# Latent attention: the outputs of two head groups joined, their sums inverted 128 rows wide and spread back by transfers, in place of transposes on VectorE

## The chip, the cores and the metric

The kernel runs on one core of a Trainium2 chip. The metric is the device time of one execution in microseconds (us). The kernel before takes 3241.66 us, the median of three executions (3239.54 to 3242.97). The core has five instruction streams that matter here: TensorE (PE; its weight loads are shown apart as PEld), VectorE (DVE), ScalarE (ACT), GpSimd (POOL) and SyncE (SP), which issues nearly all transfers (SPq in the profile). Each stream runs its instructions in order; semaphores tie them together.

## The reference, cut to what matters

The whole program is `x + attention(layernorm(x))`, followed by a two-layer local-attention block. Only the first part, a multi-head latent attention over 8 batches of 1024 tokens, is touched:

```python
D_MODEL, D_C, D_R, NH = (256, 128, 32, 16); HD = D_MODEL // NH        # HD = 16
x = L0_attn_x                                    # (8, 1024, 256), float32
c_kv = x @ W_kv_down
k_rope = _rotary_apply(c_kv @ W_k_rope, cos, sin)
k = (c_kv @ W_k_up).reshape(Bb, Tt, NH, HD)
v = (c_kv @ W_v_up).reshape(Bb, Tt, NH, HD)
q = (x @ W_q).reshape(Bb, Tt, NH, HD)
q_rope = _rotary_apply(x @ W_q_rope, cos, sin)
scores = jnp.einsum('bqhd,bkhd->bhqk', q, k)
scores = scores + jnp.einsum('bqr,bkr->bqk', q_rope, k_rope)[:, None]
scores = jnp.where(causal[None, None], -jnp.inf, scores / math.sqrt(HD + D_R))
w = jax.nn.softmax(scores, axis=-1)
attn = jnp.einsum('bhqk,bkhd->bqhd', w, v).reshape(Bb, Tt, D_MODEL)
return attn @ W_o
```

What the change touches is the division by the softmax's sum and the way from the weighted values to `attn @ W_o`.

## The kernel before

**Tiling.** The scores are held transposed: keys lie on the 128 partitions, queries along the free axis. The 16 heads form four groups `g` of four; a matmul of the values (L486) puts head `n` of a group on rows 32n to 32n+31 of a PSUM bank of 512 queries. Of these 32 rows the first 16 are the head's values and row 16 is the sum of its weights, since the value tile carries a column of ones after each head (`VW = 17`). The queries come in two halves, `c = 1` (512 to 1023) and `c = 0`.

**Steps.** The work of one batch is a list of 36 units (`units`, L595): first `c = 1`, groups 0 and 1 (units 0 to 12) and groups 2 and 3 (13 to 25), then `c = 0`, groups 0 and 1 (26 to 30) and groups 2 and 3 (31 to 35). A unit is a block of 128 keys, or two short blocks together. In step `s` the program emits, for each engine in this order: the scores of unit `s` (L453, TensorE) and their exponents (L461, ScalarE, two 128x1024 instructions); the product of unit `s-1` with the exponents of the position scores (`turned`, L475, VectorE, two 128x1024 instructions); the matmuls of unit `s-2` with the values (`values`, L486, TensorE). Then come the pieces of other work that the table `beside` (L542) hangs on step `s`: projections of this batch and of the next one, statistics, and the output matmuls `out_add` (L528) with the sum into `x` on VectorE (L532) and its store (L533). The order of PE, DVE, ACT and POOL is the order in which the program emits them (`manual_schedule`); SP's transfers are placed by the framework, and SP takes them one after another. Step 0 of a batch follows step 35 of the one before without a gap, so the last units of a batch are finished in the first steps of the next. After the last batch eleven steps without units follow.

**The end of a group.** When a group's last unit is through `values` (steps 13 and 14 for the first pair of groups, 26 and 27, 31 and 32, and steps 0 and 1 of the next batch), ScalarE copies the bank to `oaT`. One step later `finished` runs on VectorE: a transpose in blocks of 32x32 (L502), which brings queries to the partitions and a head's 17 numbers beside each other; the reciprocal of the 16 sums per row (L504); the product (L508), which writes 16 columns of each head into a tile shared by the even and the odd group. One step later again, for the odd group, `turn_back` transposes the joined tile (L516) to `oT`, whose 128 rows are the channels of eight heads. `out_add` uses `oT` as the stationary operand against `wout`. The output blocks of `c = 1` hang on steps 31, 35 and 0 of the next batch, those of `c = 0` on steps 6 and 10 of the next batch. In the last batch the `c = 1` blocks are held back to the first step after the units.

**Transfers on SP in this stage.** Per batch there are 16 L368 (256 KB each, `q` spread over partitions) and 16 L383 (128 KB each, the same for `k`), four L533 (256 KB stores of `x`) and two L189 (512 KB loads of `x`). `q` and `k` are cast on ScalarE into a high and a low half; the low half comes from a second matmul (`low`, L353).

Of the kernel before, what the change touches and what calls it, by code (L numbers as in the profile page):

```python
# [36 lines left out]
P = 128  # L37
# [11 lines left out]
VW = HD + 1  # L49
# [33 lines left out]
def preln_mla_local_kernel(  # L83
# [72 lines left out]
    def mla(ctx: ExitStack, verdict):  # L156
# [96 lines left out]

        norms = wp.tile([P, B], F32, name="norms")
# [3 lines left out]
        class Batch:  # L258
# [178 lines left out]
            def start(self):  # L437
                b = self.b
                self.rs = small.tile([P, 2, 4, 16], F32, tag="rs", name=f"rs{b}")
                self.acc, self.onat, self.oTs, self.adds = {}, {}, {}, {}  # L440
# [36 lines left out]
            def values(self, parts, pts):  # L477

                lo, ended = 0, []
                for c, g, kb in parts:  # L480
                    q0, w, _ = self.block(c, kb)
                    if kb == 0:
                        self.acc[g] = pacc.tile([P, 512], F32, tag=f"acc{g % 2}", name=f"acc{self.b}_{c}_{g}")
                    for n in range(4):
                        h = 4 * g + n
                        nc.tensor.matmul(  # L486
                            self.acc[g][32 * n : 32 * n + 32, q0 - c * 512 :],
                            self.v[:, kb, h * VW : h * VW + 32], pts[n // 2][:, n % 2, lo : lo + w],
                            start=(kb == 0), stop=(kb == 4 * c + 3),
                        )  # L490
                    lo += w
                    if kb == 4 * c + 3:
                        oT = late.tile([P, 512], F32, tag="oaT", name=f"oaT{self.b}_{c}_{g}", bufs=2)
                        on_a(oT, self.acc.pop(g))
                        ended.append((c, g, oT))
                return ended

            def finished(self, c, g, oT):


                nat = late.tile([P, 16, 32], F32, tag="onat", name=f"onat{self.b}_{c}_{g}", bufs=2)
                nc.vector.transpose(nat.rearrange("p b d -> p (b d)"), oT)  # L502
                r = self.rs[:, c, g]
                nc.vector.reciprocal(r, nat[:, :, HD])  # L504
                e = g % 2
                if e == 0:
                    self.onat[c, g // 2] = nat
                nc.vector.tensor_tensor(  # L508
                    self.onat[c, g // 2][:, :, HD * e : HD * e + HD], nat[:, :, :HD],
                    r.unsqueeze(2).to_broadcast([P, 16, HD]), ALU.mult,  # L510
                )

            def turn_back(self, c, g):
                if g % 2:
                    t = late.tile([P, 512], F32, tag="oT", name=f"oT{self.b}_{c}_{g}", bufs=3)
                    nc.vector.transpose(t, self.onat.pop((c, g // 2)).rearrange("p b d -> p (b d)"))  # L516
                    self.oTs[c, g // 2] = t
                if (c, g) == (0, 3):
                    verdict(self.rs.rearrange("p c g b -> p (c g b)"), f"a{self.b}")
# [22 lines left out]
        for step, who, *what in (  # L542
# [31 lines left out]
            (31, 0, "out_add", 4, 0), (31, 0, "out_add", 4, 1),  # L574
            (32, 1, "rotary", 1, 3),
            (33, 1, "rotary", 1, 2),
# [33 lines left out]
        line, done, turning = [], [], []  # L610
        with tc.manual_schedule(engines={E.PE, E.DVE, E.Activation, E.Pool}):
            for b in range(B + 1):
                for step in range(len(units) if b < B else 11):
# [23 lines left out]
                    if turning:  # L637
                        bt, e = turning.pop(0)
                        bt.turn_back(*e)
                    if done:  # L640
                        bt, e = done.pop(0)
                        bt.finished(*e)
                        turning.append((bt, e[:2]))
                    done += ended
# [1245 lines left out]
```

## Time and profile before

| | |
|---|---|
| time, median of 3 | 3241.66 us (3239.54 to 3242.97) |
| the profiled execution | 3241.02 us |
| its span in the trace | 3239.2 us |
| latent attention | about 0 to 945 us, a batch every 111.4 us |
| local attention and its feed-forward | about 945 to 3239 us |

The profile is of one execution. A busy share counts the time in which an engine had an instruction; TensorE's ends are modelled, so a full TensorE may still have slack. A row of a timeline gives the start, the duration (of neighbouring like instructions together), the engine, the line of the kernel, the operation, the tiles, shapes, the count and, in brackets, how long the engine stood idle before it and what ended that.

The groups of the changed part, over the whole stage on VectorE (line, operation, count, busy time, mean):

| line | what | count | busy us | mean ns |
|---|---|---|---|---|
| L475 | product with the position exponents, 128x1024 | 576 | 672.5 | 1219 |
| L502 | transpose to queries on partitions, 128x512 | 64 | 45.0 | 703 |
| L504 | reciprocal, 128x16 | 64 | 16.2 | 254 |
| L508 | product with the reciprocals, 128x256 | 64 | 27.2 | 425 |
| L516 | transpose back, 128x512 | 32 | 22.5 | 704 |

### The profile page before, as it was taken

Reading aid. Unit: us, or ns where it says so; the run is one execution under the profiler, and the core shown is the slowest. Engines: PE = TensorE matmul, PEld = TensorE weight load, DVE = VectorE, ACT = ScalarE, POOL = GpSimd, SP = SyncE. Lnnn points to the kernel's source line nnn. Section 1 sums busy time; section 2 is a strip of 40 time slices with the busy share of each in tenths; the row PEclk is TensorE's granted clock in tenths of the full one; section 3 lists DMA queues with packets and bytes.
Section 4 is the critical chain, followed back from the end, with each engine's and each line's share of the span. In section 5 each row is a group of like instructions: output and inputs, shape, how many; then the busy total and the mean of one; then the engine's idle time right before and its main releaser. Section 6 shows DMA issues by size and latency. Waiting matters only on the chain.

```text
span 3239.2 us, 112711 instructions
## 1 busy us (share of the span) xinstructions
PE 3159.7 (98%) x50210; PEld 1462.9 (45%) x50210; DVE 2648.5 (82%) x3934; ACT 1734.7 (54%) x2183; POOL 1355.6 (42%) x1065
## 2 busy tenths in 40 slices
PE   7999999999987999999999999999999999999998
PEld 2434444434333454444454444445444444454454
DVE  4999999999988888787888877787877788787773
ACT  6888888888742434444444444443444444444441
POOL 1111010100027655555655654555565555555540
PEclk9999999999998999999999999999999999999999
DMA  4133222422434354544445446455544545454431
GB/s 134 43 93 86 63 73 76 105 51 68 114 95 108 108 132 123 135 112 126 126 118 132 115 130 158 119 136 139 148 123 130 134 122 141 131 147 122 117 107 56
DMA packets 389901, 364.21 MB, mean 112 GB/s; under 512 B 158703, under 2 KB 337310, under 8 KB 389278
## 3 DMA queue, kind: packets, MB, share of 16 engines
q1 hardware_dynamic: 387422, 354.51, 41.3%
q8 instruction: 396, 6.49, 0.8%
q10 hardware_dynamic: 1984, 2.41, 0.2%
q14 instruction: 99, 0.81, 0.1%
HBM read 165.96 MB, written 140.51 MB: 95 GB/s over the span
## 4 chain that ended last, share of the span: by engine, by line
PE 91%; DVE 4%; DMA 2%; ACT 1%; POOL 1%; SPq 1%; issue 1%; DVEq 0%; ACTq 0%
PE ag L668 18%; PE pair L668 13%; PE psy L668 10%; PE acc L486 9%; PE psw L668 7%; PE sc L453 6%; PE pv L668 6%; PE o L1001 6%; PE pair L960 5%; PE psR L201 2%; PE psx L201 2%; PE psq L201 2%; PE s L1009 2%; PE psc L201 1%; PE psrq L201 1%; PE psv L201 1%
## 5 line engine op out<-in xcount | busy, mean ns | idle before, releaser
L475 DVE TENSOR_TENSOR pt<-pt,er 128x1024 f32<-128x1024 f32 x576 | 672.5, 1219 | 13.4 <-ACT pt L461 13.1
L668 PE MATMUL ag<-d,l 128*32 128x512 f32 x5632 | 639.6, 593 | 1.5 <-DVE xs L1041 1.1
L904 POOL TENSOR_TENSOR t<-t,t 128x1024 f32<-128x1024 f32 x128 | 304.2, 2376 | 798.4 <-DVE t L900 798.4
L461 ACT ACTIVATE pt<-sc 128x1024 f32<-128x1024 f32 x576 | 561.8, 1035 | 92.7 <-PE sc L453 83.3
L966 ACT ACTIVATE pt<-pair 128x1024 f32<-128x1024 f32 (+1 forms) x256 | 235.2, 969 | 537.4 <-PE pair L960 480.2
L668 PE MATMUL pair<-l_qkv,xT 128*32 128x512 f32 x4096 | 468.7, 597 | 3.6 <-DMA xT<-zx 2.6
L126 POOL TENSOR_TENSOR rn<-ss,half 128x16 f32<-128x16 f32 x128 | 373.0, 2914 | 13.8
L486 PE MATMUL acc<-pt,v 128*32 128x512 f32 (+3 forms) x3072 | 342.3, 496 | 6.4 <-DVE pt L475 6.3
L668 PEld LDWEIGHTS ag<-d,l 128*32 128x32 f32 x5632 | 177.4, 110 | 373.9 <-issue 354.3
L895 ACT ACTIVATE sq<-pair 128x1024 f32<-128x1024 f32 x128 | 131.3, 1026 | 352.7 <-issue 299.9
L668 PE MATMUL psy<-l,hid 128*32 128x256 f32 x5120 | 282.1, 379 | 0.0
L668 PEld LDWEIGHTS pair<-l_qkv,xT 128*32 128x32 f32 x4096 | 130.9, 111 | 305.9 <-issue 281.4
L453 PE MATMUL sc<-q,k 32*128 32x512 f32 (+3 forms) x3072 | 248.8, 381 | 8.5 <-ACT pt L461 8.3
L897 DVE TENSOR_TENSOR t<-pair,l_cos 128x1024 f32<-128x1024 f32 x128 | 156.0, 1219 | 121.6 <-ACT sq L895 121.3
L418 POOL TENSOR_SCALAR_AFFINE_SELECT er<-er 128x128 f32<-128x128 f32 x64 | 51.1, 802 | 481.1 <-ACT er L416 481.1
L1133 DVE SCALAR_TENSOR_TENSOR hid<-ag,l_b,ge 128x512 f32<-128x512 f32 x160 | 116.8, 730 | 162.6 <-ACT ge L1132 93.4
L910 POOL TENSOR_TENSOR t<-t,rn 128x1024 f32<-128x1024 f32 x128 | 243.5, 1902 | 10.0
L1001 PEld LDWEIGHTS o<-pt,v 128*32 128x32 f32 x7680 | 215.1, 110 | 66.2 <-issue 53.2
L668 PE MATMUL pv<-l_qkv,xT 128*32 128x512 f32 x2048 | 243.8, 592 | 0.0
L668 PE MATMUL psw<-l_o,oT 128*32 128x256 f32 x4096 | 236.5, 382 | 0.7 <-DVE xs L1170 0.7
L1019 DVE RECIPROCAL rs<-s 128x256 f32<-128x256 f32 x128 | 223.2, 1744 | 16.2 <-PE s L1009 16.2
L1001 PE MATMUL o<-pt,v 128*32 128x128 f32 x7680 | 234.5, 273 | 1.7 <-POOL pt L968 1.6
(326 smaller groups left out, 4595.9 us busy)
## 6 DMA issues: line engine op xcount, KB each, us to landing
z<-turned SPq DMA_DIRECT2D x512, 128.0 KB
qkT<-z SPq DMA_DIRECT2D x128, 512.0 KB
y<-xs SPq DMA_DIRECT2D x128, 128.0 KB
h<-y SPq DMA_DIRECT2D x32, 512.0 KB
zx<-turneds SPq DMA_DIRECT2D x120, 128.0 KB
xT<-zx SPq DMA_DIRECT2D x240, 64.0 KB
zh<-turnedh SPq DMA_DIRECT2D x120, 128.0 KB
d<-zh SPq DMA_DIRECT2D x30, 512.0 KB
```

The lines of the kernel that those rows point to most:

```text
L126: nc.gpsimd.tensor_tensor(out_, in_, half[:, :n], ALU.pow)
L201: nc.tensor.matmul(out[four], w[:, four], rhs, start=start, stop=stop)
L453: nc.tensor.matmul(two[n // 2][:, n % 2, lo : lo + w], k[rows], q[rows, h], start=(h == 1), stop=(h == 0),)
L461: nc.scalar.activation(pt, sc, AF.Exp, scale=SCALE)
L475: nc.vector.tensor_tensor(t, t, er.to_broadcast([P, 1024 // w, w]), ALU.mult)
L486: nc.tensor.matmul(self.acc[g][32 * n : 32 * n + 32, q0 - c * 512 :], self.v[:, kb, h * VW : h * VW + 32], pts[n // 2][:, n % 2, lo : lo + w],
L668: nc.tensor.matmul(out[four], w[:, four], rhs, start=start, stop=stop)
L904: nc.gpsimd.tensor_tensor(t1, t1, t2, ALU.add)
L910: nc.gpsimd.tensor_tensor(t1, t1, rn.unsqueeze(3).to_broadcast([P, 2, HEADS, DH]), ALU.mult)
L966: nc.scalar.activation(pt[:, :, : n * P], flat[:, :, : n * P], AF.Exp, scale=-1.0)
L1001: nc.tensor.matmul(o[32 * j : 32 * j + 32, g, a, :], vs[m][:, h * DH + a * 32 : h * DH + a * 32 + 32], pts[m][g][:, place(j), off : off + ...
L1019: nc.vector.reciprocal(rs, s)
```

## The change

The value matmul of an odd group takes its 32 columns of the value tile 16 earlier: its values then fall on rows 16 to 31 of each head's 32 rows and, since the column before a head is a column of ones, the sum falls on row 15. For an even group nothing moves. ScalarE copies an even group's bank straight into `oT` and an odd group's into a tile `odd`. SP then moves, for each group, the four rows of sums (512 numbers each) to 32 rows of 16 in a small tile `rs`; for the odd group it also moves the four blocks of 16 value rows over `oT`'s rows 16 to 31. Two steps after the odd group's end, `inverse` takes the reciprocal of both groups' sums at once on VectorE (128x32), SP stores them to DRAM (`zr`), and eight loads spread each row of 512 over the 16 partitions of its head (`by`). Four steps after the odd group's end, `scaled` multiplies `oT` by `by` on VectorE. In the table of other work the first output block of `c = 1` moves from step 31 to step 33, and a position block (`rotary 1, 2`) from step 33 to step 31.

```diff
+        zrs = [dram.tile([2, 4, 32, 16], F32, tag=f"zr{i}", name=f"zr{i}") for i in range(2)]
...
-                self.rs = small.tile([P, 2, 4, 16], F32, tag="rs", name=f"rs{b}")
-                self.acc, self.onat, self.oTs, self.adds = {}, {}, {}, {}
+                self.rs = small.tile([P, 2, 2, 2, 16], F32, tag="rs", name=f"rs{b}")
+                self.acc, self.by, self.oTs, self.adds = {}, {}, {}, {}
...
+                    at = HD * (g % 2)
...
-                            self.v[:, kb, h * VW : h * VW + 32], pts[n // 2][:, n % 2, lo : lo + w],
+                            self.v[:, kb, h * VW - at : h * VW - at + 32], pts[n // 2][:, n % 2, lo : lo + w],
...
-                        oT = late.tile([P, 512], F32, tag="oaT", name=f"oaT{self.b}_{c}_{g}", bufs=2)
-                        on_a(oT, self.acc.pop(g))
-                        ended.append((c, g, oT))
+                        self.ended(c, g)
+                        ended.append((c, g))
...
-            def finished(self, c, g, oT):
-                nat = late.tile([P, 16, 32], F32, tag="onat", name=f"onat{self.b}_{c}_{g}", bufs=2)
-                nc.vector.transpose(nat.rearrange("p b d -> p (b d)"), oT)
-                r = self.rs[:, c, g]
-                nc.vector.reciprocal(r, nat[:, :, HD])
+            def ended(self, c, g):
                 e = g % 2
-                if e == 0:
-                    self.onat[c, g // 2] = nat
-                nc.vector.tensor_tensor(
-                    self.onat[c, g // 2][:, :, HD * e : HD * e + HD], nat[:, :, :HD],
-                    r.unsqueeze(2).to_broadcast([P, 16, HD]), ALU.mult,
-                )
-
-            def turn_back(self, c, g):
-                if g % 2:
-                    t = late.tile([P, 512], F32, tag="oT", name=f"oT{self.b}_{c}_{g}", bufs=3)
-                    nc.vector.transpose(t, self.onat.pop((c, g // 2)).rearrange("p b d -> p (b d)"))
+                if e:
+                    t = late.tile([P, 512], F32, tag="odd", name=f"odd{self.b}_{c}_{g}")
+                else:
+                    t = late.tile([P, 512], F32, tag="oT", name=f"oT{self.b}_{c}_{g}", bufs=4)
                     self.oTs[c, g // 2] = t
-                if (c, g) == (0, 3):
-                    verdict(self.rs.rearrange("p c g b -> p (c g b)"), f"a{self.b}")
+                on_a(t, self.acc.pop(g))
+                for n in range(4):
+                    row = 32 * n + HD - e
+                    nc.sync.dma_start(
+                        self.rs[32 * n : 32 * n + 32, c, g // 2, e], t[row : row + 1].rearrange("o (p f) -> o p f", f=16)
+                    )
+                if e:
+                    for n in range(4):
+                        rows = slice(32 * n + HD, 32 * n + 32)
+                        nc.sync.dma_start(self.oTs[c, g // 2][rows], t[rows])
+
+            def inverse(self, c, m):
+                r = self.rs[:, c, m]
+                nc.vector.reciprocal(r, r)
+                z = zrs[m]
+                nc.sync.dma_start(z.rearrange("e n p f -> (n p) e f"), r)
+                t = self.by[c, m] = late.tile([P, 512], F32, tag="by", name=f"by{self.b}_{c}_{m}", bufs=2)
+                for n in range(4):
+                    for e in range(2):
+                        lo = 32 * n + HD * e
+                        nc.sync.dma_start(
+                            t[lo : lo + HD], z[e, n].rearrange("p f -> (p f)").partition_broadcast(HD)
+                        )
+                if (c, m) == (0, 1):
+                    verdict(self.rs.rearrange("p c m e f -> p (c m e f)"), f"a{self.b}")
+
+            def scaled(self, c, m):
+                t = self.oTs[c, m]
+                nc.vector.tensor_tensor(t, t, self.by.pop((c, m)), ALU.mult)
...
-            (31, 0, "out_add", 4, 0), (31, 0, "out_add", 4, 1),
+            (31, 1, "rotary", 1, 2),
             (32, 1, "rotary", 1, 3),
-            (33, 1, "rotary", 1, 2),
+            (33, 0, "out_add", 4, 0), (33, 0, "out_add", 4, 1),
...
-                    if turning:
-                        bt, e = turning.pop(0)
-                        bt.turn_back(*e)
-                    if done:
-                        bt, e = done.pop(0)
-                        bt.finished(*e)
-                        turning.append((bt, e[:2]))
-                    done += ended
+                    for what in due:
+                        what[0] -= 1
+                    while due and due[0][0] == 0:
+                        due.pop(0)[1]()
+                    for bt, (c, g) in ended:
+                        if g % 2:
+                            due.append([2, lambda bt=bt, c=c, g=g: bt.inverse(c, g // 2)])
+                            due.append([4, lambda bt=bt, c=c, g=g: bt.scaled(c, g // 2)])
+                            due.sort(key=lambda what: what[0])
```

## The prediction

> **What bounds the kernel now.** I read the page's shares first, then its busy time by stretch, then VectorE's order of time inside the attention stage, last the queue of transfers (SPq).
>
> ```profile
> PE 3159.7 (98%) x50210; PEld 1462.9 (45%) x50210; DVE 2648.5 (82%) x3934; ACT 1734.7 (54%) x2183; POOL 1355.6 (42%) x1065
> ```
>
> TensorE looks full over the whole span, but its ends are modelled. The changed code lies in the first 945 us, so the share there decides. These rows give start:end, length, then busy time of PE, PEld, DVE, ACT, POOL for the last two thirds of one batch:
>
> ```profile
> 426.00:470.00 44.00, 43.39 (x499) 17.26 (x502) 41.45 (x53) 37.99 (x50) 5.60 (x6) 1.00 0.21 49
> 470.00:512.00 42.00, 42.00 (x491) 17.32 (x483) 40.67 (x56) 34.56 (x46) 4.47 (x6) 1.00 0.20 52
> ```
>
> A batch takes 111.4 us (the L533 store of 476.64 returns at 588.02), and VectorE has 105 us in it. From 470 to 512 it is the fuller of the two eltwise engines, at 40.67 of 42. In order of time it runs without a gap:
>
> ```profile
> 494.08 0.70 DVE L502 STREAM_TRANSPOSE onat<-oaT 128x512 f32<-128x512 f32 x1
> 494.82 0.25 DVE L504 RECIPROCAL rs<-onat 128x16 f32<-128x16 f32 x1
> 495.11 0.42 DVE L508 TENSOR_TENSOR onat<-onat,rs 128x256 f32<-128x256 f32 x1
> 495.46 2.35 DVE L475 TENSOR_TENSOR pt<-pt,er 128x1024 f32<-128x1024 f32 x2
> ...
> 501.37 0.71 DVE L516 STREAM_TRANSPOSE oT<-onat 128x512 f32<-128x512 f32 x1
> ...
> 509.22 2.35 DVE L475 TENSOR_TENSOR pt<-pt,er 128x1024 f32<-128x1024 f32 x2
> 511.49 0.68 DVE L532 TENSOR_TENSOR x<-psx,x 128x512 f32<-128x512 f32 x1
> ```
>
> The reader is to see that here the group work that the change removes stands between two L475, and that L475 is what the next `values` matmul (L486) waits for. The exponent of the unit that L475 takes at 509.22 started at 504.55: VectorE is 3.6 us behind. At steps 9 and 18 of a batch (407.5, 434.5) it starts within 0.03 us of the first exponent's end. So TensorE and ScalarE set the pace in most steps (about 3.0 us each), VectorE in the last five steps of a batch and the first seven of the next. TensorE's own work in the stretch from the scores of step 31 (472.16) to those of step 7 of the next batch (511.41) is some 3.2 us less than its 39.25 us: steps 34, 4, 5 and 6 took 4.0, 4.1, 3.2 and 4.4 us, for matmuls of 3.3, 3.1, 2.4 and 3.7.
>
> **What is removed and added on VectorE.** Per batch go eight L502 (0.703), eight L504 (0.254), eight L508 (0.425) and four L516 (0.704): 13.9 us. Four reciprocals of 128x32 come; between 0.254 us for 16 columns and 1.744 us for 256 (L1019) a straight line gives 0.35. Four products of 128x512 come, 0.67 by L1024's row. That is 4.1 us, so 9.8 us of work less. In steps with no VectorE lag this is worth nothing: what hides it is the exponents. In the stretch above it is worth at most the 3.2 us that TensorE could save.
>
> **What is added on SP.** Each pair of groups issues 4+4 sum rows, 4 odd-row moves, 1 store of the inverses and 8 spreading loads: 21 transfers, 84 per batch. Rows for the price of an issue:
>
> ```profile
> 5.54 7.45 SPq L226 DMA_DIRECT2D wout<-in_L_attn_W_o_dram  x8
> ...
> 501.16 5.42 SPq L383 DMA_DIRECT2D k<-alves_place_k(1, 0)_6163  x4
> ```
>
> ```profile
> 963.27 1.77 SPq L931 DMA_DIRECT2D z<-turned  x4
> 967.08 0.34 SPq L935 DMA_DIRECT2D qkT<-z  x1
> ```
>
> L226 has 16 partitions like the spreading loads; its unhindered issues follow each other every 0.47 us (0.42 and a gap), L931's every 0.44. I take 0.47. The ends are 0.28 (the one-row stores of L690: 0.83 for three) and 1.27 (the fourth L368 of a burst). The second fence also prices a store to DRAM and the load that waits for it: the last L931 ends at 965.04 and L935 starts at 967.08, 2.04 later, 2.4 from its start; the same wait was 3.7 us for a 256 KB L533 before L189 (414.13 to 417.79). By the semaphore increments in the trace, an L226 load landed 1.9 us after its start. So I take 2.4 for the store and 1.9 for a last landing, with 3.7 as the upper end of each.
>
> One chain is then: copy; four sums (3 x 0.47 + 1.9 = 3.3); reciprocal 0.35; store 2.4; eight loads (7 x 0.47 + 1.9 = 5.2); product 0.7. That is 12 us, for a slot four steps after the copy. `scaled` stands in VectorE's order ahead of the next L475, so when it waits, L475 and then L486 wait behind it.
>
> [...]
>
> **The four pairs of a batch**, on the clock of the batch above, in the order in which the changed kernel's instructions are built:
> - Keys half 1, groups 0 and 1 (copy at step 14, about 424): loads land at 435.9, VectorE arrives near 434, next L475 at 436.6 instead of 434.5. Its L486 runs at 439.3 anyway. 0 us, at worst 1.
> - Groups 2 and 3 (copy ends 464.0): SP still owes three pieces of `k`, so sums leave 464.4 to 466.3, odd rows to 468.2, and four pieces of the next batch's `k` stand ahead of the store, to 470.5. Store lands 472.9, loads leave 473.0 to 476.8, the last lands 478.2. VectorE has ended unit 30's L475 at 475.25: 3.0 us of waiting, unit 31's L475 at 478.9 instead of 476.53, its first half ready at 480.1. TensorE wants it at 478.3 (the change exchanges 1.7 us of output matmuls in step 31 for 0.86 of position matmuls). About 2 us late; the second output block now follows in step 33.
> - Half 0, groups 0 and 1: copy 478.4, reciprocal at its slot 486.6, landing 494.6, VectorE there at 492.6. It waits 2.0, unit 0's L475 starts 495.3; TensorE wants its first half at about 496.2. Hardly a loss: TensorE stays 2.1 behind.
> - Half 0, groups 2 and 3: store at about 503, but the loads stand behind three pieces of `k` (L383), one of which needs the low halves that ScalarE casts in step 4: 504.4 before, 505.3 now. Loads leave 506.4 to 510.1 and land at 511.6; product till 512.3. Step 6's output matmuls read it at once:
>
> ```profile
> 508.76 2.30 PE L201 MATMUL psx<-wout,oT 128*32 128x256 f32 x30
> ```
>
> They now start at 512.3, last 1.7, and the scores of step 7 begin at 514.4 instead of 511.41. **A transition costs 3.0 us**, the whole saving being eaten by the waits. The `q` and `k` that SP delays are wanted eight or more steps later, and cost nothing.
>
> There are seven transitions: 21 us. The last batch has no next one to hide behind:
>
> ```profile
> 936.36 0.70 DVE L502 STREAM_TRANSPOSE onat<-oaT 128x512 f32<-128x512 f32 x1
> ...
> 939.17 5.16 PE L201 MATMUL psx<-wout,oT 128*32 128x256 f32 x56 [6.08 <-DVE oT L516]
> ```
>
> There VectorE loses 6.8 us of group work after 899, gains 2.0, and waits some 3: the last copy comes at about 931.3 instead of 933.3. From it the bare chain counts, with two loads of the next stage between: sums 935.2, store 937.9, loads out 938.8 to 942.6, landing 944.1, product 944.8. The 5.16 us of matmuls start at 944.8 instead of 939.2, before the next stage's first: 5.7 us.
>
> Sum: 7 x 3.0 + 5.7 = 26.7. The span of 3239.2 becomes 3266; the profiled execution's 3241.02 becomes 3267.7, and as it lies 0.6 below the median of 3241.66, I forecast **3268 us**.
>
> Bounds of a transition: with the last pair alone waiting, the cast of step 4 would fall at 501.8 and step 7 at 510.8, -0.6; with 0.28 an issue -1.9; no wait at all -3.2. With 3.7 for store and landing, upstream 3.1 later and 1.8 more at the end: +6 or so, as part of it meets lag that is already there.
>
> **Rivals.**
> 1. The chain is short enough (faster). Place: `scaled` at steps 31, 0 and 5. Price: 3.2 us a transition, and nothing in the last batch, where 3 us of waits and 2.3 of issues fall from the 5.7: 3241.7 - 22.4 = 3219. It decides where the last load lands before VectorE arrives, so if the chain is 3 us shorter than my 12 (0.28 an issue gives 2.0 of it). For it: VectorE's gapless 470 to 512; an engine that is behind finds its loads landed. Against: step 6's matmuls are gated by `k`'s place in SP's order, whatever VectorE does.
> 2. A wash: only that last gate acts, -0.6 x 7 + 5.7 = +1.5, so 3243. For it: the half-0 pair before it costs me almost nothing already.
> 3. SP becomes the bound. Three pairs fall between 455 and 513: 63 x 0.47 = 30 us beside the 17 us of `q`, `k` and stores, 47 of 58. At 1.27 each it would be 97, about 39 too many, less SP's free stretch after it: some +20 a transition, 3390. Against: 1.27 was seen for 256 KB transfers in a burst, while these move 2 to 32 KB.
>
> **Chances.** Forecast 0.62, rival one 0.20, the wash 0.12, SP as bound 0.06. Beyond 0.2% (6.5 us, about what three runs can tell from no change) that makes faster 0.20, same 0.12, slower 0.68. The forecast's own range is 3248 (where sameness ends) to 3296: +6 a transition, and in the tail 5.7 + 4.9 with 3.7 for its store and its two landings, give 3294. Down to 3222 the wash and the upper half of rival one come in; the rest below, and SP as bound, are what is left out.
>
> **What will show it.** In the page after: VectorE's busy time down by about 78 us with the span up; idle time before the new 128x512 product, released by the loads, near 3.0, 2.0 and 2.4 us at steps 31, 0 and 5; SP issues every 0.47 us; step 7's scores 3 us later in each batch. If instead the product starts without idle time, or the batch is under 111.4 us, the chain's length is what I had wrong; if SP never stands idle from 455 to 513, the third rival is right.

## The result, and the profile after

The changed kernel takes 3363.3 us, the median of five executions (3361.41 to 3367.48), against 3241.66 us for the kernel before in the same session: a ratio of 1.0384, 95% interval [1.0373, 1.0396]. The forecast was 3268 us, with a range of its own of 3248 to 3296 (down to 3222 with the wash and part of the first rival). The direction is right, the size is not: 121.6 us are lost where 26.7 had been worked out.

From the page after, the engines' busy time and the engines' shares of the chain of waits, then these shares from the page before:

```profile
PE 3186.7 (95%) x50210; PEld 1474.7 (44%) x50210; DVE 2582.8 (77%) x3774; ACT 1732.5 (51%) x2183; POOL 1358.6 (40%) x1065
...
PE 76%; DMA 8%; DVE 6%; SPq 5%; ACT 2%; issue 2%; POOL 1%; DVEq 0%; ACTq 0%
```

```profile
PE 91%; DVE 4%; DMA 2%; ACT 1%; POOL 1%; SPq 1%; issue 1%; DVEq 0%; ACTq 0%
```

VectorE is 65.7 us less busy, and the span is 126.5 us longer (3365.7). The chain now passes through transfers (DMA, 8%) and through SP's issuing (SPq, 5%); both were at 2% or less. The groups of instructions say who stood still (busy time, mean ns of one, idle time just before them, and what ended it); the second fence is the values' matmul before:

```profile
L488 PE MATMUL acc<-pt,v 128*32 128x512 f32 (+3 forms) x3072 | 347.6, 512 | 50.9 <-DVE pt L476 49.9
L538 DVE TENSOR_TENSOR oT<-oT,by 128x512 f32<-128x512 f32 x32 | 22.1, 692 | 127.5 <-DMA by<-zr 89.7 <-DMA rs<-oT 37.8
L523 DVE RECIPROCAL rs<-rs 128x32 f32<-128x32 f32 x32 | 11.2, 348 | 35.5 <-DMA rs<-odd 35.5
```

```profile
L486 PE MATMUL acc<-pt,v 128*32 128x512 f32 (+3 forms) x3072 | 342.3, 496 | 6.4 <-DVE pt L475 6.3
```

`scaled` (L538) waits 127.5 us in 32 uses for the spread inverses. The row puts 37.8 of these down to `rs<-oT`, moves that SP issues just behind the loads; in the one at 546.74 below, the last spreading load had landed 0.2 us earlier (at 546.52, by the counts of the semaphore that tells of a landing), so there too the loads are what it waits for. The reciprocal (L523) waits 35.5 us for the sums, and the values' matmuls (L488) have 50.9 us of idle time before them, where they had 6.4.

VectorE's order of time over one transition, the changed instructions alone:

```profile
516.12 0.35 DVE L523 RECIPROCAL rs<-rs 128x32 f32<-128x32 f32 x1 [1.62 <-DMA rs<-odd]
527.78 0.69 DVE L538 TENSOR_TENSOR oT<-oT,by 128x512 f32<-128x512 f32 x1 [6.03 <-DMA by<-zr]
538.62 0.34 DVE L523 RECIPROCAL rs<-rs 128x32 f32<-128x32 f32 x1
546.74 0.69 DVE L538 TENSOR_TENSOR oT<-oT,by 128x512 f32<-128x512 f32 x1 [1.93 <-DMA rs<-oT]
554.16 0.34 DVE L523 RECIPROCAL rs<-rs 128x32 f32<-128x32 f32 x1
567.15 0.69 DVE L538 TENSOR_TENSOR oT<-oT,by 128x512 f32<-128x512 f32 x1 [5.26 <-DMA by<-zr]
```

The waits of `scaled` at steps 31, 0 and 5 are 6.03, 1.93 and 5.26 us; forecast were 3.0, 2.0 and 2.4. Over all seven transitions they are 5.8 to 6.7, 0.9 to 2.6 and 3.8 to 7.2. SP's order over the same stretch:

```profile
510.51 1.82 SPq L384 DMA_DIRECT2D k<-alves_place_k(0, 0)_5763  x3
512.42 2.45 SPq L513 DMA_DIRECT2D rs<-odd  x4
514.92 2.49 SPq L519 DMA_DIRECT2D oT<-odd  x4
517.83 2.83 SPq L384 DMA_DIRECT2D k<-alves_place_k(0, 1)_5864  x4
520.75 0.54 SPq L525 DMA_DIRECT2D zr<-rs  x1
522.68 3.62 SPq L530 DMA_DIRECT2D by<-zr  x8
...
553.27 3.15 SPq L369 DMA_DIRECT2D q<-alves_place_q(1, 1)_6312  x4
556.52 1.11 SPq L525 DMA_DIRECT2D zr<-rs  x1
557.73 3.10 SPq L384 DMA_DIRECT2D k<-alves_place_k(1, 0)_6379  x3
561.72 3.55 SPq L530 DMA_DIRECT2D by<-zr  x8
```

The reader is to see the distance between the reciprocal and its store. The reciprocal of 516.12 is done at 516.47, and the store `zr` leaves at 520.75: 4.3 us, in which SP issues odd rows and four pieces of `k` that came earlier in its order. Four on-chip moves take 2.45 us, a transfer every 0.62.

TensorE's order of time, its two gaps in this transition:

```profile
529.67 2.20 PE L488 MATMUL acc<-pt,v 128*32 128x512 f32 x6 [4.67 <-DVE pt L476]
...
567.89 2.79 PE L201 MATMUL psx<-wout,oT 128*32 128x256 f32 x24 [5.24 <-DVE oT L538]
```

And the windows around the second gap (start:end, length, busy time of PE, PEld, DVE, ACT and POOL, the granted clock, the DMA share, GB/s):

```profile
563.00:567.00 4.00, 0.00 (x0) 0.00 (x0) 0.00 (x0) 2.02 (x3) 0.43 (x3) 0.85 0.38 88
567.00:571.00 4.00, 3.11 (x25) 1.28 (x25) 3.21 (x4) 0.00 (x0) 0.00 (x0) 0.50 0.01 2
571.00:575.00 4.00, 4.00 (x33) 1.43 (x32) 4.00 (x5) 2.99 (x4) 0.00 (x0) 0.79 0.65 165
```

This was in no step of the forecast: after the gap TensorE is granted half its clock (0.50), and it is back at full speed 6.8 us after the clock fell (565.84 to 572.66). In the middle of the stage (up to 870 us) the clock records of the trace add up to 78.5 us at half clock; the kernel before has none there.

Where in a batch the time is lost is told by ScalarE's exponents: the interval from the first exponent of a unit to that of the next, as a mean over the second to the seventh batch, less the same interval of the kernel before. The table sums these over stretches of units, in us per batch, for all kernels that were run (a batch before takes 111.4).

| kernel | units 31-34 | 35-3 | 4-8 | 20 | others | batch |
|---|---|---|---|---|---|---|
| after | +7.18 | +0.82 | +5.49 | +1.36 | +0.04 | +14.89 |
| 1: product by a constant | -0.69 | +1.22 | +2.37 | 0.00 | +0.02 | +2.93 |
| 2: matmuls in the gaps | +6.03 | +1.20 | +2.96 | +1.66 | 0.00 | +11.85 |
| 3: later product | -1.77 | +3.95 | +2.22 | 0.00 | +0.77 | +5.17 |
| 4: one spreading load | +6.28 | -0.07 | +5.17 | +0.78 | +0.12 | +12.29 |
| 5: 10 transfers, not 21 | +1.17 | -0.15 | +2.33 | +0.99 | +0.17 | +4.51 |
| 6: 10 transfers, later | -1.79 | +1.17 | -2.29 | 0.00 | +0.77 | -2.14 |
| 7: as 6, one unit more | -1.86 | +1.17 | -2.01 | 0.00 | +0.79 | -1.90 |
| 8: reciprocal of a constant too | -0.69 | -0.22 | +5.91 | 0.00 | +0.05 | +5.05 |
| 9: as 7, last batch as before | -1.86 | +1.17 | -2.21 | 0.00 | +0.75 | -2.15 |
| 10: as 8 without on-chip moves | -0.69 | -0.42 | -1.95 | 0.00 | +0.01 | -3.05 |

### The profile page after: what moved, and what is told of

It reads as the page before. It is cut to its first block, busy times and chain, and to the rows that moved or that the text cites. A ratio compares the mean times of both kernels' runs of the same rounds, so it can differ in the third digit from the quotient of the medians.

```text
span 3365.7 us, 113703 instructions
## 1 busy us (share of the span) xinstructions
PE 3186.7 (95%) x50210; PEld 1474.7 (44%) x50210; DVE 2582.8 (77%) x3774; ACT 1732.5 (51%) x2183; POOL 1358.6 (40%) x1065
## 4 chain that ended last, share of the span: by engine, by line
PE 76%; DMA 8%; DVE 6%; SPq 5%; ACT 2%; issue 2%; POOL 1%; DVEq 0%; ACTq 0%
PE ag L688 18%; PE pair L688 12%; PE psy L688 9%; PE psw L688 6%; PE pv L688 6%; PE o L1021 6%; PE acc L488 5%; PE pair L980 4%; PE sc L454 3%; DVE pt L476 2%; SPq L530 2%; ACT pt L462 2%; PE psx L201 2%; DMA zr<-rs 2%; PE s L1029 2%
## 5 line engine op out<-in xcount | busy, mean ns | idle before, releaser
L488 PE MATMUL acc<-pt,v 128*32 128x512 f32 (+3 forms) x3072 | 347.6, 512 | 50.9 <-DVE pt L476 49.9
L454 PE MATMUL sc<-q,k 32*128 32x512 f32 (+3 forms) x3072 | 253.7, 387 | 11.4 <-ACT pt L462 11.2
L1039 DVE RECIPROCAL rs<-s 128x256 f32<-128x256 f32 x128 | 223.1, 1743 | 15.7 <-PE s L1029 15.6
```

Source lines behind the costliest of these rows:

```text
L454: nc.tensor.matmul(two[n // 2][:, n % 2, lo : lo + w], k[rows], q[rows, h], start=(h == 1), stop=(h == 0),)
L488: nc.tensor.matmul(self.acc[g][32 * n : 32 * n + 32, q0 - c * 512 :], self.v[:, kb, h * VW - at : h * VW - at + 32], pts[n // 2][:, n % 2, ...
L1039: nc.vector.reciprocal(rs, s)
```

## The experiments

Theory A: the waits of the product for the spread inverses hold TensorE, and the half clock after each gap adds to it. The rivals: SP's queue and the traffic cost by themselves (B); the clock costs nothing (C); the waits only move (D); landing, not issuing, decides (E). Times are medians, ratios are to the kernel before on the same chip.

### 1. The product by a constant

```diff
-                nc.vector.tensor_tensor(t, t, self.by.pop((c, m)), ALU.mult)
+                self.by.pop((c, m))
+                nc.vector.tensor_tensor(t, t, wout.rearrange("p n d -> p (n d)"), ALU.mult)
```

> The product of the joined outputs is taken with a constant of the same size (the output weights) in place of the spread inverses, so the inverse sums are left out of the output; every transfer, the reciprocal and the product stay. What goes is the product's wait for the spreading loads. Theory A (that wait holds TensorE, about 4.7 us twice a batch at steps 31 and 5, and the half clock after each gap takes 3.4 us more, 16 us a batch in all): 3363 - 8 x 16 = 3235, between 3215 and 3260; half-clock time falls from 163 us to 50-60. Rival B (the 21 transfers of a pair load the queue of SP and the memory, so the next batch's loads and bfloat16 weights come late): no less than 3330, since they are all still there.

3275.55 us, 1.0107 [1.0090, 1.0124]. This is above A's 3260 and well below B's 3330. The kernel leaves the inverse sums out of its output. A batch loses 2.93 us instead of 14.89, so the product's wait is 12.0 of the 14.9 us. The half clock up to 870 us falls from 78.5 to 13.7 us (over the whole execution from 163.4 to 80.9, where 50 to 60 were expected). What is left shows in VectorE's waits between 150 and 850 us (total, times, longest):

```profile
DVE rs L523 <- DMA rs<-odd: 52.8, 23, 4.2
```

In the changed kernel this was 19.2 us in 10 times: with the product's wait gone, the reciprocal waits for the sums instead. ScalarE waits too: once in each of these batches its cast of `q(0, 0)` stands for 4.5 to 5.5 us until the pieces of `q(1, 1)` have left; run 8 takes this up.

### 2. Matmuls in the gaps

```diff
...
+                if parts[0] == (0, 2, 0):
+                    warm = bank(f"warm{self.b}")
+                    for _ in range(5):
+                        times(warm, wout[:, 0, :P], wout.rearrange("p n d -> p (n d)"), True, True)
...
+                if t == i == 0:
+                    for _ in range(10):
+                        times(ps[:, 0], wout[:, 0, :P], wout[:, 0, :], True, True)
```

> Matmuls whose results are overwritten are put into TensorE's two gaps: five of 512 columns ahead of the values of unit 31 and ten of 256 columns ahead of the output matmuls of step 7, some 4.3 us each at full clock; waits, transfers and VectorE's work are as in the changed kernel. Theory A (half clock after each gap costs 3.4 us, twice a batch): TensorE has more work and the kernel is faster, 3363 - 8 x 6 = 3315, between 3300 and 3335, with the half-clock time near 60 us. Rival C (only the waits count, the lower clock falls in time that is lost anyway): 3363 or above, up to 3400 where the added matmuls run past the end of the waits.

3344.47 us, 1.0325 [1.0307, 1.0343]: 19 us faster than the changed kernel, with some 9 us more of matmuls in every batch. TensorE's order shows the added work in the place of the gap, and the rest of the wait behind it:

```profile
515.46 4.50 PE L201 MATMUL warm<-wout 128*32 128x512 f32 x40
520.94 1.76 PE L492 MATMUL acc<-pt,v 128*32 128x512 f32 x6 [0.98 <-DVE pt L476]
```

There is no half clock left in the middle of the stage. C falls: the clock does cost. But A's 3300 to 3335 is missed too: the batch gains 14.89 - 11.85 = 3.0 us, half of what A had put down. That VectorE, late by the same wait, would have held TensorE in most of the slow time anyway is a reading that no run shows by itself.

### 3. The later product

```diff
-                            due.append([4, lambda bt=bt, c=c, g=g: bt.scaled(c, g // 2)])
+                            due.append([6, lambda bt=bt, c=c, g=g: bt.scaled(c, g // 2)])
...
-            (6, -1, "out_add", 0, 0), (6, -1, "out_add", 0, 1), (6, 0, "low"), (6, 1, "normalise", 0, 3),
+            (6, 0, "value", 3), (6, 0, "low"), (6, 1, "normalise", 0, 3),
...
-            (9, 0, "value", 3), (9, 0, "low"), (9, 1, "normalise", 1, 2),
+            (9, -1, "out_add", 0, 0), (9, -1, "out_add", 0, 1), (9, 0, "low"), (9, 1, "normalise", 1, 2),
...
+            (35, 0, "out_add", 4, 0), (35, 0, "out_add", 4, 1),
```

> The product is due six units after the pair's end in place of four, and what reads it moves behind: the output groups of the second half batch to steps 35 and 0/1 of the next batch, those of the first to steps 9 and 10, one value step and two rotary blocks change places with them. Transfers and work are the same, each with 6 us more to land. Theory A: both gaps go, 3363 - 128 = 3235 less what the reciprocal and product save VectorE, 3210 to 3250. Rival B (SP's queue and the traffic are the cost): over 3300, since the queue is as full. Rival D (the waits only move: the output groups meet the query and value steps and their bfloat16 copies): 3260 to 3320, with gaps of over 3 us before lines other than the values.

3295.41 us, 1.0169 [1.0152, 1.0186]. A's 3210 to 3250 is missed; the time lies in D's range and just under B's bound. The stretch of units 31 to 34 is mended (+7.18 becomes -1.77) and so is unit 20; units 4 to 8 keep 2.22 of 5.49, and units 35 to 3 lose more than they did (+3.95, of which run 6, with the same table of other work, keeps 1.17). VectorE's waits:

```profile
DVE rs L523 <- DMA rs<-odd: 28.8, 18, 3.0
...
DVE oT L538 <- DMA by<-zr: 11.9, 8, 2.4
DVE rs L523 <- DMA oT<-odd: 11.6, 4, 3.5
...
DVE oT L538 <- DMA rs<-oT: 8.0, 4, 2.5
```

The product's wait has shrunk to 19.9 us (11.9 and 8.0) from 89.5 in the same stretch of the changed kernel; the sums come late, because on SP they stand behind the spreading loads of the pair before. ScalarE's cast of `q(0, 0)` waits here as well, 2.7 to 4.0 us in five of six batches, for pieces of `q(1, 1)`. Two units more do not mend it while SP has 21 transfers for each pair.

### 4. One spreading load

```diff
-                for n in range(4):
-                    for e in range(2):
...
+                nc.sync.dma_start(
+                    t, z.rearrange("n e p f -> (n e) (p f)").unsqueeze(1).to_broadcast([8, HD, 512])
+                )
```

> The eight spreading loads of a pair become one transfer with the same bytes, the store of the inverses two in place of one, so that the last load is issued 7 x 0.46 - 0.5 = 2.7 us earlier. Theory A, with SP's issue time as the price: both waits of the product shrink by 2.7 us, from 6.0 and 5.3 to 3.3 and 2.6; with the gaps at TensorE then near 2 us no half clock follows: 16 - 4 = 12 us a batch less, 3265; if the half clock still follows, 8 x 5.4 = 43 less, 3320. Rival E (the time from issue to landing decides, and one big transfer lands later than eight small ones, or the loads stand behind other traffic): 3350 or above.

3348.80 us, 1.0338 [1.0321, 1.0356], only 14.5 us less than the changed kernel, just short of E's 3350; both of A's figures, 3265 and 3320, are missed, and 68.3 of the 78.5 us at half clock remain. That no half clock follows a gap near 2 us was the author's estimate, and it was not shown. SP's order shows where the rest stays:

```profile
505.51 2.49 SPq L519 DMA_DIRECT2D oT<-odd  x4
508.10 3.60 SPq L384 DMA_DIRECT2D k<-alves_place_k(0, 1)_5786  x4
511.80 1.21 SPq L526 DMA_DIRECT2D zr<-rs  x2
514.45 0.63 SPq L528 DMA_DIRECT2D by<-zr  x1
```

The reciprocal here ran from 506.64 to 506.99, and its store waited until 511.80 for its turn: 4.8 us. A product that waits starts 3.9 us (median) after the one load's issue, and 2.1 us after the last of the eight in the changed kernel. So of the 3.0 us of issuing that are saved (eight loads took 3.6 us, one takes 0.63) the landing gives 1.8 back, and the second store 0.6.

### 5. Ten transfers for a pair in place of 21

Beside the one spreading load, a group's four sums go to DRAM in one transfer and come back 128 rows wide in one.

```diff
-                for n in range(4):
-                    row = 32 * n + HD - e
...
+                nc.sync.dma_start(zss[m][e], t[HD - e : P : 32])
                 if e:
...
+                    nc.sync.dma_start(self.rs[:, c, m], zss[m].rearrange("e n (p f) -> (n p) e f", f=16))
```

> A pair of groups issues 10 transfers in place of 21: each group's four sums go to DRAM in one, come back 128 rows wide in one, the inverses go out in two and are spread in one; the odd rows keep their four. SP's issue time per pair falls from about 12 x 0.63 + 0.5 + 8 x 0.46 = 11.7 us to about 10 x 0.55 = 5.5 us, but the sums now make a round trip through DRAM (some 2 x 1.8 us) in place of one landing. Theory A with SP's issue time as the price: 3348 (one spreading load, measured) less 0 to 3 us a batch, 3322 to 3350. Rival E (each transfer's time from issue to landing decides, and there are now more of them in a row): the reciprocal waits some 2 us longer in every pair, four times a batch of which two or three reach TensorE, 3370 to 3400.

3293.59 us, 1.0159 [1.0141, 1.0177]. This is better than either theory: 55 us less than with one spreading load, for an exchange of eight on-chip moves for three transfers that make a longer way. SP's order:

```profile
599.65 1.23 SPq L385 DMA_DIRECT2D k<-alves_place_k(0, 1)_7142  x2
600.98 1.18 SPq L525 DMA_DIRECT2D zr<-rs  x2
603.59 0.63 SPq L527 DMA_DIRECT2D by<-zr  x1
```

The reciprocal of this pair ran from 599.69 to 600.04 and the store leaves at 600.98: 0.9 us instead of 4.8. For the pairs at this place the first seven batches show 0.8 to 2.0 us here and 3.4 to 5.1 in run 4. E falls: the chain has one landing more and is faster. What fell is the time that its links stand in SP's order; eight on-chip moves held SP for some 5 us, the three transfers in their place hold it for 1.6.

### 6 and 7. Both, and one unit more

Run 6 is run 5 with the places of run 3; run 7 has the reciprocal three units after the pair's end and the product seven.

```diff
-                            due.append([2, lambda bt=bt, c=c, g=g: bt.inverse(c, g // 2)])
-                            due.append([6, lambda bt=bt, c=c, g=g: bt.scaled(c, g // 2)])
+                            due.append([3, lambda bt=bt, c=c, g=g: bt.inverse(c, g // 2)])
+                            due.append([7, lambda bt=bt, c=c, g=g: bt.scaled(c, g // 2)])
```

> The 10 transfers of the run before together with the later product and the later output groups. Theory A: what is left in the run with the later product alone (5.1 us a batch more than before: waits of the reciprocal and of the product for loads that stand behind other transfers on SP) goes in part, 3295 - 8 x 3 = 3270, between 3245 and 3290. Rival E: the reciprocal's longer wait costs what the product's gains, 3290 to 3330.

> The same 10 transfers and places of the output groups, the reciprocal three units after the pair's end in place of two and the product seven in place of six: one more unit (3 us) for the sums to land. Theory A with the reciprocal's wait as the rest: VectorE waits nowhere for a transfer in the middle of the stage, a batch takes 111.4 - 2.7 (the steps 4, 31, 34 and 35 that the changed kernel already does faster) = 108.7 to 111.4, and the time is 3240 less 0 to 19 plus 12 to 18 at the end of the last batch, 3235 to 3260. Rival E: over 3280.

3245.24 us, 1.0017 [1.0007, 1.0026], and 3242.34 us, 1.0009 [1.0000, 1.0019]. A holds in both, run 6 at the lowest end of its 3245 to 3290. The unit more takes the reciprocal's wait between 150 and 850 us from 30.8 us in 18 times to 0.2 in one, yet the batch gets no shorter (-2.14 and -1.90): in run 6 VectorE waited where TensorE did not need it. The windows of one batch, of the changed kernel and then of run 6, in two fences:

```profile
542.60:669.30 126.70, 115.24 (x1288) 47.55 (x1288) 97.03 (x111) 96.44 (x129) 11.69 (x14) 0.95 0.34 81
```

```profile
479.50:589.10 109.60, 108.73 (x1285) 45.24 (x1288) 96.36 (x112) 96.56 (x128) 14.37 (x14) 1.00 0.38 94
```

The same matmuls; 11.5 us without them and a clock of 0.95 in the first, 0.9 us without them and a full clock in the second. A batch is now 2 us shorter than the kernel before has it. Nothing of that reaches the whole: the end of the stage, where no next batch hides the chain, takes it back. From the last exponent to the next stage's first matmul 33.4 us pass in run 6 and 20.0 before, and the units of the last batch take 5.7 us more than before.

### 8. Reciprocal and product by constants

The product's edit is that of run 1; beside it:

```diff
-                r = self.rs[:, c, m]
-                nc.vector.reciprocal(r, r)
+                r = small.tile([P, 2, 16], F32, tag="inv", name=f"inv{self.b}_{c}_{m}", bufs=4)
+                nc.vector.reciprocal(r, wout.rearrange("p n (a f) -> p (n a) f", f=16)[:, :2])
```

> As the run with the product by a constant, and the reciprocal too reads a constant: neither the sums nor the spread inverses enter the output, all 21 transfers of a pair are issued, and VectorE waits for none of them before the product (only for the odd rows). Theory A (the waits of VectorE are the whole loss in the middle of the stage): a batch takes 108.7 to 110, less than before's 111.4, and the time is 3240 - 8 x 2 + 13 at the end = 3237, between 3225 and 3250. Rival B (the queue of SP costs by itself): the batches stay above 113 and the time above 3265.

3290.66 us, 1.0156 [1.0136, 1.0177]. It is slower than run 1, although one wait more was taken away: B was right here. VectorE's waits for transfers are down to 4.0 us between 150 and 850 us, so they are not the cause. TensorE, ScalarE and SP in order of time, three views of this kernel:

```profile
527.50 0.79 PE L354 MATMUL psq<-alves_place_q(0, 0)_6474,minus 128*128 128x512 f32 x1 [3.81 <-ACT alves_place_q(0, 0)_6474 L79]
```

```profile
526.87 0.59 ACT L79 CAST alves_place_q(0, 0)_6474<-psq 128x512 fp32r<-128x512 f32 x1 [7.25 <-DMA q<-alves_place_q(1, 1)_6327]
```

```profile
511.31 2.42 SPq L513 DMA_DIRECT2D rs<-oT  x4
...
514.46 2.40 SPq L513 DMA_DIRECT2D rs<-odd  x4
516.90 3.04 SPq L519 DMA_DIRECT2D oT<-odd  x4
520.05 3.12 SPq L369 DMA_DIRECT2D q<-alves_place_q(1, 1)_6327  x4
```

Read from the bottom: `q(1, 1)` was cast by 511.99 (its second cast starts at 511.40 and takes 0.59), but twelve on-chip moves stand ahead of its four pieces, which leave from 520.05. The cast tile has two buffers (`halves`, L348, `bufs=2`), so ScalarE can't cast `q(0, 0)` before those pieces are read: it stands for 7.25 us, the low half's matmul (L354) waits for it, and the scores after that. (These casts write `fp32r`, as the row says; the copies that two of the expectations call bfloat16 are no part of this kernel.)

### 9. The last batch as before

Run 7, with VectorE's transposes in the last batch alone.

```diff
...
+                if self.b == B - 1:
+                    if e:
+                        self.finished(c, g - 1, self.first)
+                    self.first = oT = late.tile([P, 512], F32, tag="odd", name=f"oaT{self.b}_{c}_{g}")
+                    on_a(oT, self.acc.pop(g))
+                    if e:
+                        due.append([2, lambda: self.finished(c, g, oT)])
+                        due.append([3, lambda: self.turn_back(c, g // 2)])
+                    return
...
```

> The run with 10 transfers and the latest product, with the last batch alone done by VectorE's transposes as in the kernel before. Theory A (in the middle a batch gains 2.2 us on before; the last batch and the joint to the next stage lose 5 and 10 us, since nothing is left there to hide the chain of transfers): 3242 - 5 - 8 = 3229, between 3222 and 3236, faster than both kernels. Rival F (the loss at the joint comes from something else, such as the next stage's first loads): 3236 to 3245.

3226.72 us, 0.9955 [0.9942, 0.9969]: faster than both kernels, and F falls. The new way in the last batch was worth 3242.34 - 3226.72 = 15.6 us. TensorE's last wait in the stage, in run 7 and in this one:

```profile
942.53 4.97 PE L201 MATMUL psx<-wout,oT 128*32 128x256 f32 x56 [12.40 <-DVE oT L535]
```

```profile
924.67 5.51 PE L201 MATMUL psx<-wout,oT 128*32 128x256 f32 x56 [4.79 <-DVE oT L519]
```

From the last exponent to the next stage's first matmul it is 32.3 us in run 7 and 19.6 here, as before the change (20.0).

### 10. Without most on-chip moves

```diff
-                for n in range(4):
-                    row = 32 * n + HD - e
...
                 if e:
-                    for n in range(4):
...
+                    nc.sync.dma_start(self.oTs[c, g // 2][HD:32], t[HD:32])
+                nc.gpsimd.memset(self.rs[:, c, g // 2, e], 1.0)
```

> As the run in which product and reciprocal read constants, but 11 of the 12 on-chip moves of a pair (the sums, three of the four moves of odd rows) are left out too, so neither the sums, the inverses nor most odd rows enter the output; SP keeps the store and the eight spreading loads. Theory B' (in that run SP's queue, not VectorE, held TensorE: the low part of the queries waited for its place to be emptied behind 12 moves of 0.62 us): the batch falls from 116.3 to 109 to 110, the time to 3232 to 3250. Rival G (that wait is for something else, such as ScalarE's order): batches stay above 114, 3275 or more.

3216.64 us, 0.9927 [0.9912, 0.9942], beyond the expected 3232 to 3250, and the batch falls to 108.3. Against run 8 eleven of the twelve on-chip moves of a pair are gone (eight small fills on GpSimd a batch came in), so the moves are the 8.1 us a batch between the two. `q(1, 1)` leaves before the next cast needs its place:

```profile
487.27 3.12 SPq L369 DMA_DIRECT2D q<-alves_place_q(1, 1)_6183  x4
```

That is 0.03 us after its second cast ended; in run 8 it was 8.1 us. The last piece lands 4.80 us after its issue here and 4.83 in run 8, so in this transition the moves cost by their place in SP's order and not by the traffic they make. The low half of `q(0, 0)`, at 498.31, waits for nothing. This kernel also shows what VectorE's saved work (with the changed table of other work) is worth when nothing waits: 3.05 us a batch.

## Why the prediction was wrong in size

The steps that failed are the one that places the chain's links in SP's order at steps 31 and 5, the one that lets the delayed `q` and `k` cost nothing, and the one that sizes the end of the stage; the half clock was no step at all.

**What held.** VectorE's terms: the reciprocal takes 0.348 us (0.35 forecast), the product 0.692 (0.67). By the lines, VectorE's work falls by 77.8 us, as forecast; the page's 65.7 is smaller because it counts overlapping instructions once. The worth of that saving was put at 3.2 us a transition at most; run 10 gains 3.05. The places of the waits, steps 31, 0 and 5, were right, and at step 0 the size too (2.0 forecast, 1.93 measured in this transition). There two errors cancelled: the store landed in 1.6 us and not 2.4, while the eight loads took 5.9 us to the last landing and not 5.2. Right was also the issue time of a spreading load, 0.46 against 0.47.

**Step 31 failed by its place in SP's order.** The forecast's chain and the measured one, in us from the end of the odd group's copy (464.02 in the trace of before, 510.51 after):

| | forecast | measured |
|---|---|---|
| odd group's sums start to leave | 0.4 | 1.9 |
| odd rows have left | 4.2 | 6.9 |
| store of the inverses leaves | 6.5 | 10.2 |
| first spreading load leaves | 9.0 | 12.2 |
| product starts | 14.2 | 17.3 |
| VectorE ready for the product | 11.2 | 11.2 |

VectorE came when it was expected; the inverses came 3 us late, and that doubled the wait. Of it TensorE was to lose 2 us; units 31 to 34 lose 7.2, half clock included. The 3.7 us by which the store is late are three pieces of `k` ahead of the sums (1.5), eight on-chip moves at 0.62 us where 0.47 was taken from loads out of DRAM (1.2), and four pieces of `k` that took 3.3 us and not 2.3 (1.0). The price of 0.62 lies within the bounds of 0.28 to 1.27 us an issue. The third rival, "SP becomes the bound", had 0.06 and was priced only for a full SP. SP was not full. From 502 to 566 us it spent 49.7 of 64 us issuing 85 transfers (before, from 455 to 513: 16.9 of 58 us for 24), and it stood idle in between, from 534.7 to 536.5 for instance. So the queue held the chain back without being full: the wrong transfers stood ahead of the late one.

**Step 5 failed in the store's landing.** From the store's issue to the first load the forecast took 3.4 us; it was 5.2 (556.52 to 561.72). The three pieces of `k` were out by 560.83, so the last 0.9 are the store's own landing, 5.2 us after its issue and behind four 256 KB pieces of `q`. Over the seven transitions it landed after 3.7 to 5.2 us; the upper end of 3.7 was too low in four of them. VectorE was also ready 0.8 us earlier than forecast (5.4 us after the store's issue, not 6.2). The first pair of the keys' half 1, forecast at 0 and at worst 1, costs 1.36 (unit 20).

**"The `q` and `k` that SP delays are wanted eight or more steps later, and cost nothing" is false.** The tiles are wanted late, but the buffers they are cast in are wanted at the next cast. In the changed kernel the product's waits cover this; in run 8 units 4 to 8 lose 5.9 us, and run 10, without most of the moves, gains 2.0 there.

**The half clock was missing from the sum.** Run 2 gains 3.0 us a batch by keeping TensorE busy through the gaps. In the changed kernel's trace the half clock comes for 3.41, 6.83 or 10.24 us at a time, 78.5 us in all up to 870 us, and it also followed stretches in which TensorE was busy for a part of the time, as told at the end.

**The end of the stage was under-sized.** From the start of the last exponent to the next stage's first matmul the changed kernel takes 35.2 us (1037.1 to 1072.3) and the kernel before 20.0 (925.2 to 945.2): 15.2 us, where the forecast had 5.7. From the end of the last copy (1043.09) to the end of the product the forecast's chain took 13.5 us; it took 22.3. The reciprocal started 7.2 us after the copy, where 3.9 were forecast, because the even group's four moves and a second store of `x` (1043.44 to 1046.50) stood ahead of the odd group's sums. The landing was right: the last spreading load was issued at 1058.02 and had landed by 1059.70, 1.7 us later (1.9 forecast). But the product starts at 1064.75, without idle time before it, 5.0 us after its data was there. In VectorE's order the next stage's normalisation stands ahead of it, and this had waited for its own loads of `x` and for GpSimd:

```profile
1056.45 0.75 DVE L801 BATCH_NORM_STATS2 bnsts<-xs 128x6 f32<-128x256 f32 x2 [4.93 <-DMA xs<-x2d]
...
1063.45 1.38 DVE L812 TENSOR_SCALAR xs<-xs,mvs,rstds 128x256 f32<-128x256 f32 x4 [1.12 <-POOL rstds L126]
1064.75 0.68 DVE L538 TENSOR_TENSOR oT<-oT,by 128x512 f32<-128x512 f32 x1
```

The forecast had no term for this. So in the changed kernel, unlike run 9 against run 7, the next stage's first loads (rival F there) have a part in the loss.

The sum by measurement: of the loss in the profiled execution some 89 us are six middle batches of 14.9 each, 23 the first and the last batch, 15 the end of the stage. So a transition costs 14.9 us, not 3.0. Of this 12.0 go with the product's wait (run 1), the half clock that follows that wait included; the 2.9 that remain, 6.0 against what run 10 gains, are the reciprocal's wait and SP's order, which take each other's place (runs 1 and 8). Whether another queue could issue some of the 21 transfers was not tried.

## What to carry to other kernels

When work is exchanged for a chain of small transfers on one queue, price each link by what stands ahead of it in that queue at that moment, and look for the buffers that the delayed transfers keep from being reused. Here 3 us more in the queue doubled a wait, and the on-chip moves cost run 8 8.1 us a batch by their place. A wait that leaves TensorE idle for a few microseconds can be paid again in the clock (two gaps of 5 us: 3.0 us a batch). A chain that is hidden in the middle of a loop shows at its end, where the old way may be kept: with 10 transfers, a later product and the last batch left as it was, the idea gains 0.45%.

## What the runs showed of the hardware

- In the changed kernel a transfer from SBUF to SBUF holds SP for 0.59 us (median), one of 2 KB as well as one of 32 KB; a spreading load out of DRAM holds it for 0.42. In run 4 the one transfer of 256 KB that replaces eight of 32 KB holds it for 0.63, but what waits for it starts 3.9 us (median) after its issue, and in the changed kernel 2.1 after the last issue of the eight, each of which lands after 1.84 (median).
- In the changed kernel the store of the inverses (16 KB) landed 1.6 us after its issue at step 0 of a batch, and 3.7 to 5.2 us after it at step 5, behind four transfers of 256 KB.
- In the changed kernel's trace every clock record up to 880 us begins a whole number of times 3.41 us after the first. Cut into stretches of that length from 50 to 880 us, the trace has 11 at full clock in which TensorE was busy for less than 0.35 of the time; half clock followed all 11, none of the 204 above 0.70, and one of the five between (398.59 to 402.00, busy for 1.47 us). In seven traces (this one and runs 1, 3, 4, 5, 8 and 10) it followed all 35, none of 1556, and 10 of 29. So TensorE need not be idle for a whole stretch: from 439.55 to 442.96 it was busy for 1.01 us, and from 442.96 to 446.37 its clock was 0.50.
